# Horner's form with the bare square, and a second m turned out of PSUM, in a matrix square root kernel

## The chip, the cores and the metric

The kernel runs on one core of a Trainium2 chip. The metric is the device time of one execution in microseconds (us), lower is better. Engines are called as in the profile: PE is TensorE (with PEld for its weight loads), DVE is VectorE, ACT is ScalarE, POOL is GpSimd, SP is SyncE, which here only issues DMAs.

## What is computed

The input x has shape (32, 32, 128, 128): 32 images of 32 channels, each channel a 128 x 128 matrix. Layer 0 normalises groups of two channels, and then takes a matrix square root of every channel by five coupled Newton-Schulz steps; layer 1 normalises again and convolves by way of a spectrum. The change is in layer 0:

```python
normA = jnp.sqrt(jnp.sum(A2 * A2, axis=(1, 2)))
Y = A2 / normA[:, None, None]
Z = jnp.broadcast_to(I, A2.shape)
for _ in range(NUM_ITER):
    T = 0.5 * (3.0 * I - jnp.matmul(Z, Y))
    Y = jnp.matmul(Y, T)
    Z = jnp.matmul(T, Z)
sA = Y * jnp.sqrt(normA)[:, None, None]
...
x = x + _L0_conv_ref(_gn(x))
x = x + _L1_conv_ref(_gn(x), L1_conv_weights1, L1_conv_weights2)
```

## The kernel before

**Groups and lanes.** The work of layer 0 is cut into 256 groups of four channels, so a tile of a group is 128 x 512 float32. Each group is one generator, `newton`, which issues some instructions and yields. Up to eight generators (lanes) are under way; the main loop goes round all lanes, one step of each in a round, so that the instructions of eight groups are interleaved on every engine. Every instruction is kept in the order in which the program issues it. A new far group starts every 23/8 = 2.875 rounds (`FAR`). `yield from rest` is two rounds.

**Near and far.** The kernel has no five steps but two quartic polynomials and a final factor. With m the current matrix, a quartic q(m) is evaluated; y = q m; the second m is q y; another quartic of it follows; and then the products of the end. Images 1 to 18 are "far" (144 groups), the others "near" (112 groups, `near_quartic`, which uses PE transposes). Only the far groups are changed.

**The far quartic before.** `far_quartic(m, mb, v, more)` takes m, its transpose mb, and v, a multiple of the identity minus m, which POOL made ahead. TensorE makes the square from mb and m (a product takes its left factor transposed). DVE adds a multiple of the square, from PSUM, to v. The second product needs the transpose of that v as a factor. It is made in two parts: DVE's `transpose` turns every 32 x 32 block (tile `turn`, four buffers in turn), and four DMAs from SP's queue put the blocks of rows into their places in tile `w`. After two rests (four rounds) TensorE multiplies v and w, and DVE adds mb, which POOL has replaced by `eye_q` minus mb, to give q.

**Between the two quartics.** ACT takes y and, two rounds later, the second m out of PSUM (tile `my` holds both side by side). Two rounds later, `transposed(m)` lets TensorE transpose the four matrices of m, ACT copies them into `mb`, and POOL makes v. Two rounds on, the second quartic starts.

**What else runs beside it.** ACT issues the loads of x (`b`, `xt`, and `xs` for the statistics of coming images), SP the stores of the result (`mid`), of spectra (`xs<-spec`) and the `w<-turn` DMAs. DVE also makes the statistics. The later stage of the kernel does the products of layer 1 and the inverse transforms, with the near groups of images 19 to 31 beside them. All instructions pass through one helper, so that the profile gives them all line L89; they are told apart by tiles.

Of the kernel before, what the change touches and what calls it, by code (L numbers as in the profile page):

```python
# [31 lines left out]
ALU = mybir.AluOpType  # L32
# [4 lines left out]
P = 128  # L37
# [11 lines left out]
MS = 1 / QR  # L49
EYE = QD * MS * MS  # L50
QF = EYE / (36 / 16)

SV = MS / 4.5
SQ = MS / 8.625
EYE_V = 3.375 * SV
EYE_Q = 24.609375 * SQ
QS = 16 * SQ
FIRST = GROUPS[0] - 1
MORE = FIRST * 8 + 6
NB = 8  # L60
# [34 lines left out]
def conv_preact_kernel(  # L95
# [19 lines left out]
    nc.vector.tensor_scalar_mul(eye1[:, 0, :], ident, EYE)  # L115
    eye = eye1.to_broadcast([P, 4, P])
    eyes = []
    for n, f in (("v", EYE_V), ("q", EYE_Q)):
        e = const.tile([P, 1, P], F32, name=f"eye_{n}")
        nc.vector.tensor_scalar_mul(e[:, 0, :], ident, f)  # L120
        eyes.append(e.to_broadcast([P, 4, P]))
    eye_v, eye_q = eyes
    avg_mean = const.tile([P, P], F32, name="avg_mean")
    nc.vector.memset(avg_mean, -1.0 / 512)

# [97 lines left out]
    def prep(bs, made):  # L223

        n = len(bs)
        nc_, ng = n * C, n * G
        first_b = bs[0]
        st = small.tile([P, ng, 6], F32, tag="a_st", name=f"a_st{first_b}", bufs=2)
        tiles = []
        parts = [(b, i) for b in bs for i in range(C // 4)]  # L230

        ahead = 3 if first_b else 8

        def load(k):
            b, i = parts[k]
            if first_b or i < 4:
                t = stp.tile([P, 2, 2 * P], F32, tag="xs", name=f"xs{b}_{i}")
            else:
                t = four("turn", True).rearrange("p (j c) x -> p j (c x)", j=2)
            src = xs_in[b, :, 2 * i : 2 * i + 2].rearrange("p g h c -> p g (h c)")  # L240
            kept(nc.scalar.dma_start(out=t, in_=src))
            tiles.append(t)

        for k in range(ahead):
            load(k)
        yield
        for k in range(len(parts)):
            for j in range(2):
                nc.vector.bn_stats(st[:, 2 * k + j, :], tiles[k][:, j, :])
            yield  # L250
            if k + ahead < len(parts):
                load(k + ahead)
        ms = small.tile([P, ng], F32, tag="a_ms", name=f"a_ms{first_b}")
        nm, d = yield from moments(st, ms, "a")
        yield from pause
        pq = bank()[:, 0, 0:nc_]
        nc.tensor.matmul(pq, avg_mean, d.rearrange("p g c -> p (g c)"), start=True, stop=True)
        if not first_b:
            warm(5)

        v = small.tile([P, nc_ + ng], F32, tag="a_v", name=f"a_v{first_b}")
        nc.vector.tensor_scalar_mul(v[:, 0:nc_], pq, -512 / (P * P))
        yield
        vg = small.tile([P, ng], F32, tag="a_vg", name=f"a_vg{first_b}")
        nc.vector.tensor_reduce(
            vg, v[:, 0:nc_].rearrange("p (g c) -> p g c", c=2), AX.X, ALU.add
        )
        nc.vector.tensor_scalar(v[:, nc_:], vg, 0.5, EPS, ALU.mult, ALU.add)
        yield
        s = small.tile([P, nc_ + ng], F32, tag="a_r_s", name=f"a_r_s{first_b}", bufs=2)  # L270
        yield from root(v, nc_ + ng, s)
        iv = small.tile([P, nc_ + ng], F32, tag="a_inv", name=f"a_inv{first_b}")
        nc.vector.reciprocal(iv, s)
        yield

        sc = small.tile([P, nc_], F32, tag="a_sc", name=f"a_sc{first_b}", bufs=2)
        nc.vector.tensor_scalar_mul(sc, iv[:, 0:nc_], MS / P)
        off = small.tile([P, ng, 2], F32, tag="a_off", name=f"a_off{first_b}", bufs=2)
        nc.vector.tensor_tensor(
            off,  # L280
            sc.rearrange("p (g c) -> p g c", c=2),
            nm[:, :, None].to_broadcast([P, ng, 2]),
            ALU.mult,
        )
        off = off.rearrange("p g c -> p (g c)")
        sn = small.tile([P, nc_], F32, tag="a_t_s", name=f"a_t_s{first_b}", bufs=3)
        for k, b in enumerate(bs):
            g, c = slice(k * G, k * G + G), slice(k * C, k * C + C)
            made[b] = (nm[:, g], sc[:, c], off[:, c], sn[:, c])
        yield  # L290
        nn = small.tile([P, ng, 2], F32, tag="a_d", name=f"a_n{first_b}")
        nc.vector.tensor_tensor(
            nn,
            s[:, 0:nc_].rearrange("p (g c) -> p g c", c=2),
            iv[:, nc_:, None].to_broadcast([P, ng, 2]),
            ALU.mult,
        )
        nn = nn.rearrange("p g c -> p (g c)")
        for far in sorted({is_far(b) for b in bs}):
            of = [k for k, b in enumerate(bs) if is_far(b) == far]  # L300
            c = slice(of[0] * C, of[-1] * C + C)
            f = EYE_Q * QS if far else EYE * QF
            nc.vector.tensor_scalar_mul(nn[:, c], nn[:, c], P * (1.5 / f) ** 2)
        yield
        yield from root(nn, nc_, sn)
        yield
# [6 lines left out]
    def four(tag, more):  # L313
        n, m = rooms[tag]
        shape = [P, 4, 2, P] if tag == "my" else [P, 4, P]
        if more:
            turns[tag] += 1
            if turns[tag] % (n + m) >= n:
                return early.tile(shape, F32, tag=tag + "_early", name=tag, bufs=m)
        return sets.tile(shape, F32, tag=tag, name=tag, bufs=n)  # L320
# [15 lines left out]
    def blocks(t):  # L336


        return t.rearrange("p c x -> p (c x)").rearrange("p (a c j) -> p a c j", a=4, c=4)

    def minus(eye, m, t):

        nc.gpsimd.tensor_tensor(t, eye, m, ALU.subtract)
        return t

    def products(lhsT, rhs):
        ps = bank()
        for j in range(4):
            nc.tensor.matmul(ps[:, j, :], lhsT[:, j], rhs[:, j], start=True, stop=True)
        return ps  # L350
# [67 lines left out]
        yield from rest  # L418
        return q

    def far_quartic(m, mb, v, more):

        ps = products(mb, m)
        nc.vector.scalar_tensor_tensor(v, ps, 1 / (4.5 * MS), v, ALU.mult, ALU.add)
        t = four("turn", more)
        nc.vector.transpose(blocks(t), v.rearrange("p c (i b) -> p b c i", b=4))
        w = four("w", more)
        into = w.rearrange("p c x -> p (c x)").rearrange("p (a x) -> p a x", a=4)
        for a in range(4):
            src = t[32 * a : 32 * a + 32].rearrange("p c x -> p (c x)")  # L430
            kept(
                nc.sync.dma_start(
                    out=into[:, a], in_=src.rearrange("p (b x) -> p b x", b=4)
                )
            )
        minus(eye_q, mb, mb)
        yield from rest
        yield from rest
        ps = products(v, blocks(w).rearrange("p a c j -> p c a j"))
        q = plus(ps, SQ / SV**2, mb, "q", more)  # L440
        yield from rest
        return q

# [2 lines left out]
    def newton(g, sn, xt, m, mb, v, far, more):  # L446


        qf, et, eye_t = (QS, EYE_Q, eye_q) if far else (QF, EYE, eye)
        q = yield from far_quartic(m, mb, v, more) if far else near_quartic(m, mb, more)  # L450
        my = four("my", more)
        y = my[:, :, 0, :]
        nc.scalar.mul(y, products(q, m), 1 / (MS * qf))
        yield from rest
        m = my[:, :, 1, :]
        nc.scalar.mul(m, products(q, y), MS / qf)
        yield from rest
        mb = taken(transposed(m), "mb", more)
        if far:
            v = minus(eye_v, m, four("v", more))  # L460
        yield from rest
        q = yield from far_quartic(m, mb, v, more) if far else near_quartic(m, mb, more)
        both = [bank().rearrange("p (j k) x -> p j k x", k=2) for _ in range(2)]
        for j in range(4):
            nc.tensor.matmul(both[j // 2][:, j % 2], q[:, j], my[:, j], start=True, stop=True)
        w, y = four("t", more), four("y4", more)
        for h in range(2):
            nc.scalar.mul(w[:, 2 * h : 2 * h + 2, :], both[h][:, :, 1, :], 1 / (MS * qf))
        for j in range(4):
            c = 4 * g + j  # L470
            nc.scalar.mul(y[:, j, :], both[j // 2][:, j % 2, 0, :], sn[:, c : c + 1])
        yield from rest
        t = plus(products(w, q), -0.5 * et / (1.5 * qf), eye_t, "t", more)
        yield from rest
        nc.vector.tensor_tensor(xt, products(t, y), xt, ALU.add)
        if not todo and lanes.count(None) == LANES - 1:
            warm(2)
        yield
# [707 lines left out]
```

## Time and profile before

| | us |
|---|---|
| median of three runs | 3018.24 (3017.86 to 3018.54) |
| profiled execution, own time | 3016.65 |
| its span | 3014.70 |
| PE busy in 90 to 1554 us (far stage) | 1452.46 of 1464 |
| DVE busy there | 1256.10 |
| POOL busy there | 1056.15 |
| ACT busy there | 884.59 |
| share of the 16 DMA engines there | 0.58 |

The page gives busy time, share of the span and instructions of each engine, then the span in 40 slices, one digit each for tenths of busy time. Groups of instructions are written as output <- inputs, with the shapes, then the count, the busy time and the mean length of one in ns, and behind the second bar the idle time of the engine just before them and what ended it. Waits are written as engine, tile, what was waited for: total us, times, longest. In a timeline each line has a start, a length and what ran; SPq is SP's queue of DMA issues. The stretch view has busy time, with the number of instructions in brackets, for each engine, and then the granted clock, the share of the DMA engines and GB/s.

### The profile page before, as it was taken

To read this page: it belongs to the slowest core of one execution; us is meant where nothing else is said; L and a number is where in the kernel's file an instruction comes from. 1 tells how busy PE (TensorE), PEld (TensorE's weight loads), DVE (VectorE), ACT (ScalarE), POOL (GpSimd) and SP (SyncE) were. 2 spreads that over 40 slices of the span, in tenths; PEclk is the share of its full clock that TensorE was granted. 3 is DMA by queue.
4 is the path that set the end of the run, shared out by engine and by line. 5 is a ranking of instruction groups with operands and counts; after the bars stand their busy time and mean duration, and the time that the engine had idled before them with its cause. 6 is when DMAs were issued, how large, how long until landed. Compare 5 with 4: busy or idle time off the path is not lost.

```text
span 3014.7 us, 73315 instructions
## 1 busy us (share of the span) xinstructions
PE 2897.6 (96%) x27112; PEld 2689.0 (89%) x27112; DVE 2321.8 (77%) x4262; ACT 1652.1 (55%) x4187; POOL 1995.8 (66%) x2308
## 2 busy tenths in 40 slices
PE   7999999999999999999999999999989999999995
PEld 7899999999999999999999889888878899888884
DVE  7778898989888888889876645777886767776564
ACT  4566666566565656566554445455544544665452
POOL 4676777777777767777765434787777763678352
PEclk9999999999999999999999999999999999999997
DMA  5465655556565656565633566777877737676576
GB/s 176 135 176 145 171 163 153 167 152 180 134 192 135 192 131 195 142 183 140 190 102 99 158 209 208 257 247 254 271 235 245 252 121 225 203 242 216 175 230 242
DMA packets 442482, 560.91 MB, mean 186 GB/s; under 512 B 99344, under 2 KB 260112, under 8 KB 442128
## 3 DMA queue, kind: packets, MB, share of 16 engines
q1 hardware_dynamic: 328512, 347.77, 38.7%
q10 hardware_dynamic: 113616, 208.45, 22.2%
q8 instruction: 218, 3.57, 0.5%
q14 instruction: 136, 1.11, 0.1%
HBM read 326.93 MB, written 153.62 MB: 159 GB/s over the span
## 4 chain that ended last, share of the span: by engine, by line
PE 71%; POOL 8%; DVE 7%; DMA 7%; issue 5%; SPq 1%; ACT 1%; ACTq 0%; POOLq 0%; DVEq 0%
PE ps L89 71%; POOL yt L89 3%; POOL r L89 2%; POOL x L89 1%; POOL fold L89 1%; DMA yt<-mid 1%; SPq L89 1%; DVE turn L89 1%; DVE root L89 1%; DMA w<-turn 1%; DMA out<-yt 1%; DVE v L89 1%; DVE yt L89 1%; DVE a_d L89 1%; DMA xs<-in_xs 1%
## 5 line engine op out<-in xcount | busy, mean ns | idle before, releaser
L89 PE MATMUL ps<-my,q 128*128 128x128 f32 (+1 forms) x4096 | 747.0, 330 | 16.6 <-DVE q L89 9.9
L89 PEld LDWEIGHTS ps<-my,q 128*128 128x128 f32 x4096 | 623.0, 192 | 67.7 <-issue 7.4
L89 PE MATMUL ps<-w,v 128*128 128x128 f32 x4096 | 555.4, 279 | 19.6 <-DVE w L89 15.3
L89 ACT ACTIVATE b<-b,a_off,a_sc 128x128 f32<-128x128 f32 x1024 | 469.7, 491 | 166.2 <-issue 57.0
L89 ACT ACTIVATE my<-ps 128x512 f32<-128x512 f32 x512 | 306.2, 599 | 428.3 <-PE ps L89 408.9
L89 POOL TENSOR_TENSOR fold<-xt 128x256 f32<-128x256 f32 x512 | 363.4, 731 | 261.5 <-DVE xt L89 248.9
L89 PEld LDWEIGHTS ps<-w,v 128*128 128x128 f32 x4096 | 502.9, 193 | 32.5 <-DVE w L89 13.9
L89 POOL TENSOR_TENSOR yt<-yt,d 128x512 f32<-128x512 f32 x244 | 306.5, 1279 | 223.2 <-ACT d L89 195.5
L89 ACT ACTIVATE t<-ps 128x256 f32<-128x256 f32 x512 | 192.0, 381 | 311.7 <-PE ps L89 298.4
L89 DVE STREAM_TRANSPOSE turn<-v 128x512 f32<-128x512 f32 x288 | 326.1, 1132 | 9.9
L89 POOL TENSOR_SCALAR x<-xt,a_nm,a_sc 128x128 f32<-128x128 f32 x736 | 321.4, 450 | 15.6 <-DVE a_sc L89 15.4
L89 POOL TENSOR_TENSOR mb<-eye_q,mb 128x512 f32<-128x512 f32 x144 | 184.0, 1278 | 197.8 <-ACT y L89 139.2
L89 ACT ACTIVATE y<-ps,a_t_s 128x128 f32<-128x128 f32 x1024 | 290.4, 374 | 0.0
L89 POOL TENSOR_TENSOR v<-eye_v,x 128x512 f32<-128x512 f32 x144 | 184.0, 1278 | 143.8 <-ACT x L89 136.7
L89 PE MATMUL ps<-q,t 128*128 128x128 f32 x2048 | 273.9, 277 | 4.3 <-ACT t L89 3.7
L89 PE MATMUL ps<-x,b 128*128 128x128 f32 x2048 | 277.7, 279 | 0.0
L89 PE MATMUL ps<-x,q 128*128 128x128 f32 x2048 | 274.7, 277 | 3.0 <-DVE w L89 2.0
L89 DVE SCALAR_TENSOR_TENSOR v<-ps,v 128x512 f32<-128x512 f32 x288 | 195.1, 678 | 104.5 <-PE ps L89 101.8
L89 PE MATMUL ps<-y,t 128*128 128x128 f32 x2048 | 274.5, 277 | 0.1
L89 PE MATMUL ps<-my,mb 128*128 128x128 f32 x2048 | 272.2, 276 | 0.0
L89 PEld LDWEIGHTS ps<-my,mb 128*128 128x128 f32 x2048 | 257.9, 192 | 9.6 <-issue 1.6
L89 PEld LDWEIGHTS ps<-x,q 128*128 128x128 f32 x2048 | 249.4, 192 | 14.1 <-issue 8.4
(131 smaller groups left out, 5074.9 us busy)
## 6 DMA issues: line engine op xcount, KB each, us to landing
w<-turn SPq DMA_DIRECT2D x1152, 64.0 KB
b<-in_x ACTq DMA_DIRECT2D x256, 256.0 KB
xt<-in_xt ACTq DMA_DIRECT2D x256, 256.0 KB
mid<-xt SPq DMA_DIRECT2D x256, 256.0 KB
yt<-mid SPq DMA_DIRECT2D x128, 512.0 KB
xs<-in_xs ACTq DMA_DIRECT2D x252, 256.0 KB
out<-yt SPq DMA_DIRECT2D x115, 512.0 KB
plain<-in_wk SPq DMA_DIRECT2D x34, 512.0 KB
```

The costliest lines, as they stand in the source:

```text
L89: return self.tc.keep_in_program_order(issue(*args, **kw))
```

## The change

The polynomial's constants change. Before, the second factor was a shifted v, so that v itself had to be turned; now it is the bare square, which is turned straight out of PSUM, ahead of the sum into v. So `transpose` reads PSUM instead of SBUF. The second m is no longer transposed by TensorE and copied by ACT: DVE turns it out of PSUM too, after ACT has taken m from the same bank, and four DMAs put it into `mb`, 32 columns of each of the four matrices at a time, where w gets 128 contiguous columns. This starts two rounds earlier than the transposes did. The turned second m is left without ACT's factor, so that the second quartic has its own identity (`eye_p`), factor and scale. The number of rounds of a far group is the same.

```diff
-SV = MS / 4.5
-SQ = MS / 8.625
-EYE_V = 3.375 * SV
-EYE_Q = 24.609375 * SQ
-QS = 16 * SQ
+EYE_V = 3 * MS
+EYE_Q = 36 / 39 * MS
+QS = 16 / 39 * MS
+TURNED = QS / MS
...
-    for n, f in (("v", EYE_V), ("q", EYE_Q)):
+    for n, f in (("v", EYE_V), ("q", EYE_Q), ("p", EYE_Q * TURNED)):
...
-    eye_v, eye_q = eyes
+    eye_v, eye_q, eye_p = eyes
...
-            f = EYE_Q * QS if far else EYE * QF
+            f = EYE_Q * QS * TURNED**2 if far else EYE * QF
...
-    def far_quartic(m, mb, v, more):
+    def across(ps, more, into):
...
-        ps = products(mb, m)
-        nc.vector.scalar_tensor_tensor(v, ps, 1 / (4.5 * MS), v, ALU.mult, ALU.add)
         t = four("turn", more)
-        nc.vector.transpose(blocks(t), v.rearrange("p c (i b) -> p b c i", b=4))
-        w = four("w", more)
-        into = w.rearrange("p c x -> p (c x)").rearrange("p (a x) -> p a x", a=4)
+        nc.vector.transpose(blocks(t), ps.rearrange("p c (i b) -> p b c i", b=4))
         for a in range(4):
             src = t[32 * a : 32 * a + 32].rearrange("p c x -> p (c x)")
             kept(
-                nc.sync.dma_start(
-                    out=into[:, a], in_=src.rearrange("p (b x) -> p b x", b=4)
-                )
-            )
+                nc.sync.dma_start(out=into(a), in_=src.rearrange("p (b x) -> p b x", b=4))
+            )
+
+    def far_quartic(m, mb, v, more, f, eye_q):
+
+        ps = products(mb, m)
+        w = four("w", more)
+        across(ps, more, lambda a: w.rearrange("p c x -> p (c x)")[:, P * a : P * a + P])
+        nc.vector.scalar_tensor_tensor(v, ps, 1 / (9 * MS * f), v, ALU.mult, ALU.add)
         minus(eye_q, mb, mb)
         yield from rest
         yield from rest
         ps = products(v, blocks(w).rearrange("p a c j -> p c a j"))
-        q = plus(ps, SQ / SV**2, mb, "q", more)
+        q = plus(ps, 9 / (39 * MS**2), mb, "q", more)
         yield from rest
         return q
...
-        qf, et, eye_t = (QS, EYE_Q, eye_q) if far else (QF, EYE, eye)
-        q = yield from far_quartic(m, mb, v, more) if far else near_quartic(m, mb, more)
+        qf = QS if far else QF
+        if far:
+            q = yield from far_quartic(m, mb, v, more, 1.0, eye_q)
+        else:
+            q = yield from near_quartic(m, mb, more)
...
-        nc.scalar.mul(m, products(q, y), MS / qf)
-        yield from rest
-        mb = taken(transposed(m), "mb", more)
+        ps = products(q, y)
+        nc.scalar.mul(m, ps, MS / qf)
         if far:
+            mb = four("mb", more)
+            across(ps, more, lambda a: mb[:, :, 32 * a : 32 * a + 32])
+            yield from rest
             v = minus(eye_v, m, four("v", more))
-        yield from rest
-        q = yield from far_quartic(m, mb, v, more) if far else near_quartic(m, mb, more)
+            yield from rest
+            qf, et, eye_t = QS * TURNED, EYE_Q * TURNED, eye_p
+            q = yield from far_quartic(m, mb, v, more, TURNED, eye_p)
+        else:
+            yield from rest
+            mb = taken(transposed(m), "mb", more)
+            yield from rest
+            et, eye_t = EYE, eye
+            q = yield from near_quartic(m, mb, more)
```

## The prediction

> **What bounds the kernel now.** I read the page's sections 1 and 2 first, then busy time by stretch, then groups by form, then SP's waits, all of the stage that the change touches. That stage runs from the first `turn` (89.6 us) to the last (1553.3 us): 144 far groups in 1464 us, and in its even middle part (300 to 1300 us) 100 groups in 1000 us, so 10.0 us a group.
>
> ```profile
> PE 2897.6 (96%) x27112; PEld 2689.0 (89%) x27112; DVE 2321.8 (77%) x4262; ACT 1652.1 (55%) x4187; POOL 1995.8 (66%) x2308
> PE   7999999999999999999999999999989999999995
> ```
> ```profile
> core 0: us, PE busy (x) PEld busy (x) DVE busy (x) ACT busy (x) POOL busy (x), PEclk, DMA share, GB/s
> 700.00:900.00 200.00, 198.82 (x1674) 188.57 (x1673) 174.91 (x318) 120.36 (x308) 145.12 (x160) 1.00 0.59 164
> 1100.00:1300.00 200.00, 199.28 (x1682) 189.08 (x1681) 170.38 (x299) 121.67 (x313) 145.53 (x160) 1.00 0.57 156
> 2000.00:2200.00 200.00, 193.87 (x1747) 175.22 (x1746) 156.16 (x290) 106.55 (x281) 154.66 (x178) 1.00 0.80 263
> ```
>
> A busy PE proves little by itself[...]; but weight loads fill 94% too (189 of 200), the clock is granted in full, and the chain of waits inside 300 to 1300 us is 86.9% "PE ps". So TensorE is the limit of this stage. Second is VectorE: 170 to 175 of 200, or 8.64 us of each 10.0. ScalarE has 6.1, GpSimd 7.3. The third row, of the later stage, shows that a DMA share of 0.80 goes with a PE still 97% busy.
>
> The rows that the change touches (300 to 1300 us, groups by form; then the timeline of the weight loads; then SP's own waits and its issues):
>
> ```profile
> L89 DVE STREAM_TRANSPOSE turn<-v 128x512 f32<-128x512 f32 x200 | 226.5, 1132 | 6.8
> L89 PEld LDWEIGHTS ps<-ident,my 128*128 128x128 f32 x400 | 47.1, 142 | 0.0
> L89 ACT COPY mb<-ps 128x512 f32<-128x512 f32 x100 | 58.5, 585 | 30.5 <-PE ps L89 25.6 <-DVE q L89 2.2 <-DMA w<-turn 1.7
> L89 DVE STREAM_TRANSPOSE u<-ps 128x512 f32<-128x512 f32 x25 | 17.8, 710 | 2.5 <-PE ps L89 2.5
> L89 ACT COPY z<-ps 128x256 f32<-128x256 f32 x26 | 8.4, 375 | 10.4 <-PE ps L89 10.4
> L89 ACT ACTIVATE t<-ps 128x256 f32<-128x256 f32 x198 | 73.5, 379 | 91.2 <-PE ps L89 91.0
> ```
> ```profile
> 802.60 0.47 PEld L89 LDWEIGHTS ps<-ident,my 128*128 128x128 f32 x4
> 803.04 0.97 PEld L89 LDWEIGHTS ps<-w,v 128*128 128x128 f32 x8
> ```
> ```profile
> SPq L89 <- DVE turn L89: 315.5, 93, 7.0
> SPq L89 <- DVE b_v L89: 51.6, 13, 4.7
> SPq L89 <- PE ps L89: 31.4, 98, 0.8
> SPq L89 <- DMA w<-turn: 14.5, 15, 4.9
> ```
> ```profile
> 602.29 2.50 SPq L89 DMA_DIRECT2D w<-turn  x4
> 604.84 0.60 SPq L89 DMA_DIRECT2D mid<-xt  x1
> ```
>
> The reader is to see: the four transposes of a group hold TensorE 0.44 us (802.60 to 803.04); a turn out of SBUF takes 1.13 us, the one block transpose out of PSUM (`u<-ps`) 0.71; SP's waits add up to about 437 us of these 1000 (all rows of that answer), so its issues and the gaps between them take 5.63 us a group: two sets of `w<-turn` at 2.5 us and one `mid<-xt` at 0.54 to 0.60.
>
> [...] The trace speaks against a price there, on ScalarE at least: `z<-ps` reads PSUM in 16-byte steps in 375 ns, the contiguous `t<-ps` of that size takes 379. [...]
>
> **The change part by part**, per far group, against the profiled run (3016.65 us, span 3014.70; the median of the three runs, 3018.24, is 1.6 above it and takes the same difference).
>
> - TensorE loses the 4 transposes of the second m: 0.44 us, times 144 is 63.4 us. They lie on the bound, with nothing beside them; so this is the expected gain. Its bank of PSUM falls away too. Next late is VectorE, then SP.
> - ScalarE loses `mb<-ps`, 0.585 us: 6.1 becomes about 5.5. It has idle time; worth nothing.
> - VectorE has three turns out of PSUM for two out of SBUF. Unknown: the price of a 16-byte step in PSUM. Low end 0.71 (`u<-ps`, contiguous): 8.64 - 2.26 + 2.13 = 8.5 us. High end 1.13, as if the step cost as in SBUF: 9.8. I take 0.71, for the ScalarE row above. At 8.5 of 9.56 us VectorE stays second.
> - The turn now goes ahead of the sum into `v`: w's transfers can start 0.71 us after the product instead of 0.68 + 1.13 = 1.81; `v` is ready 0.71 later, but its product waits for w longer. A gain of slack, not of time. The other constants, the extra eye (one 128x128 multiply at the start) and the norm's factor: nothing.
> - SP gets 4 more issues a group, `mb<-turn`. Their access has one dimension more than w's. Low end 2.5 us a set, as w's. High end: `or<-od` against `ob<-od` (616 and 464 ns medians) puts 150 ns on one more dimension, 3.1 us. SP: 5.63 + 2.5 to 3.1 = 8.1 to 8.7 of 9.56. I take 8.3. Behind a late issue stand the next w set and `mid`.
> - DMA: a row of 32 floats per partition and block, so 128-byte packets, 2048 a group. The store `xs<-spec` has such packets: in the window of 1079.7 to 1081.7 us they were 2070 at 83.6% of 16 engines, 12.9 ns each. 2048 x 12.9 / 16 = 1.65 us a group; the share goes from 0.58 of 10.0 to (5.8 + 1.65) / 9.56 = 0.78, which the later stage bears. [...]
> - Path of the second m: before, PE to ScalarE, transposes two rounds on, ScalarE, product two rounds on. Now it has four rounds (a round is 10.0 / 2.875 = 3.5 us, then 3.3): 13.3 us against 0.6 (ScalarE) + 0.7 (turn) + 2.5 to 3.1 (issues) + 2.2 (landing, the `DMA w<-turn` pieces of the chain last 2.1 to 2.3) = 6 to 7 us, so 6 us for queueing. w has as much.
> - Two added waits. VectorE's turn of m stands behind ScalarE's `my`: queued behind it are turns and sums of other lanes, with 1.0 us of idle time a group to take it. And in the built program each DMA of SP and ScalarE takes one of eight completion semaphores in turn and waits for the DMA eight before it. It was 12 DMAs in 10.0 us, 6.7 us back; it becomes 16 in 9.56, 4.8 us back, with landings of 2.2 us upward. So ScalarE's loads can stand behind SP's sets, and its evacuations behind its loads. The before shows little of it: 14.5 us in 1000 on SP, about 10 on ScalarE. Bounds: nothing, or up to 0.6 us a group, past the gain. I take 0.07 us a group, 10 us: TensorE's idle time in this stage is 11.5 us now (1452.5 busy of 1464), and I let it double.
>
> Sum: -63.4 + 10 = -53; 3018.2 - 53 = 2965 us. Own range 2950 to 2998: from nothing given back with some earlier start, to two thirds of the gain given back.
>
> **The rivals.**
> 1. SP and its ring of eight become the bound (slower). For: SP at 87 to 91% before any wait, three sets per group of which two come close together, TensorE's operands for two of eight products behind it, four `turn` buffers that VectorE must wait for. Against: both paths have 6 us of slack, and the before waited little. Price: 8.7 + 1.6 us of landing waits = 10.3 us a group, +0.3 x 144 = 43: 3061 us. It decides from the point where SP's issues and waits pass 10.0 us a group; between 9.56 and 10.0 it only eats the gain.
> 2. The step in PSUM costs as in SBUF, and VectorE is the bound. [...] Against: `z<-ps`. Price: 9.77 us of work plus 0.4 of waits that stay = 10.2: +25, 3043 us; with no waits left, 2985.
> 3. The gain is eaten by both in part: 9.9 to 10.05 us a group, 3004 to 3025, 3014 in the middle.
> 4. The change doesn't do what it says: excluded for the transposes, which are missing in the changed program's list of TensorE; SP's list has the four new issues a group.
>
> **How the numbers follow.** Forecast 0.58; rival 1 0.22; rival 2 0.12, of which 0.08 slower, 0.02 the same and 0.02 faster; rival 3 0.08, of which 0.03 faster, 0.03 the same, 0.02 slower. About 0.2% (6 us) is what a measurement of this kernel can tell from no change. Faster 0.58 + 0.02 + 0.03 = 0.63, the same 0.05, slower 0.22 + 0.08 + 0.02 = 0.32. The range starts at 2948 (all of the gain, and a little of the startup) and reaches into rivals 1 and 2, to 3060, which leaves out half of rival 1 and the forecast's edges, under 0.2. The forecast's own range stands beside it: 2950 to 2998.
>
> **What would show each step.** Right: the stretches of 200 us hold 20.9 groups instead of 20, PE still at 199; `ps<-ident,my` 448 instead of 1024; `turn<-ps` at 0.71 us; VectorE near 177 of 200; `mb<-turn` issues at 0.60 to 0.75 us and SP's wait for `turn` at a third of before; DMA share 0.75 to 0.8. Wrong: `turn<-ps` over 1 us; SP with hardly a wait for `turn` and long ones for DMAs; ScalarE's `my` or `b` waiting for `mb<-turn`; PE below 195 of 200 with "DMA mb<-turn" or "DVE turn" as releaser. The forecast fails if any of these costs TensorE 0.44 us a group.

## The result, and the profile after

The changed kernel takes 3039.67 us (median of 5 runs, 3030.63 to 3042.62), the one before, on the same chip, 3018.54 (3017.86 to 3020.63). The ratio is 1.0066, with a 95% interval of 1.0049 to 1.0083: slower by 21 us, where 53 us of gain were forecast. The profiled execution took 3030.63 us, 9 under the median, so its trace shows rather too little of the loss; its span is 3028.5.

First the page's sections 1 and 2 of the kernel after, then its busy time by stretch, in the columns that the prediction's fence has.

```profile
PE 2856.4 (94%) x26536; PEld 2636.7 (87%) x26536; DVE 2271.7 (75%) x4407; ACT 1567.5 (52%) x4043; POOL 1995.5 (66%) x2308
PE   7999999999999999999999999999989999999996
```
```profile
700.00:900.00 200.00, 189.43 (x1537) 177.40 (x1536) 161.60 (x329) 105.84 (x285) 141.75 (x156) 0.99 0.75 187
1100.00:1300.00 200.00, 190.90 (x1562) 179.72 (x1561) 162.49 (x314) 108.94 (x290) 143.53 (x158) 1.00 0.74 183
2000.00:2200.00 200.00, 193.96 (x1736) 175.21 (x1735) 156.42 (x292) 107.06 (x280) 156.74 (x177) 0.99 0.78 256
300.00:1300.00 1000.00, 954.87 (x7803) 897.99 (x7803) 814.06 (x1602) 541.54 (x1440) 715.51 (x789) 0.99 0.74 185
```

TensorE has lost its transposes, yet it works less of each stretch: 189 of 200 us, where it was 199. The tenths of section 2 don't show it, as 95% is a 9 too. The last `turn` ends the stage at 1567.3 us, 14 later than before; the later stage (2000 to 2200) is as it was. From one `t` of a group to the next the mean is 10.17 us (10.01 before), with 98.3 groups in 1000 us. So TensorE is busy 954.87 / 98.3 = 9.71 us a group and idle 0.46. Before it was 995.62 / 99.9 = 9.97 and 0.04. Without the 0.44 of the transposes 9.53 should be left: 0.18 us of the loss hide inside "busy", and 0.42 are new idle time.

A part of the 0.18 is the granted clock. From 300 to 1300 us it was 1.00 throughout before. After, it falls to half in four stretches of 3.41 us, and each begins 0.5 to 1.2 us after TensorE has come back from a pause of 2.0 to 3.6 us. The longest such pause and the stretch behind it, in the same columns:

```profile
855.57:859.12 3.55, 0.00 (x1) 0.04 (x1) 3.55 (x9) 0.00 (x0) 1.67 (x3) 1.00 0.93 293
859.98:863.39 3.41, 3.41 (x19) 3.41 (x18) 1.38 (x2) 3.41 (x11) 0.20 (x1) 0.50 0.67 155
```

The other three begin at 518.65, 549.37 and 1006.76 us. TensorE counts as busy in all four, so they hide 6.8 us of work at full clock at most, 0.07 us a group. Two more pauses over 2 us (2.27 and 2.33 us, at 391 and 1165 us) have no such stretch behind them. The other 0.11 us are not explained.

Of the chain of waits inside 300 to 1300 us, 86.9% was "PE ps" before. Now it is 41.6%, and DMAs and SP's issues make up another third (the line's first entries):

```profile
by line: PE ps L88 41.6%; SPq L88 10.6%; DMA w<-turn 8.8%; DMA mb<-turn 8.5%; DMA mid<-xt 4.4%; DVE turn L88 3.1%; issue 2.7%; DVE v L88 2.2%; DMA xs<-in_xs 1.8%; ACT b L88 1.6%; DVE q L88 1.6%; POOL v L88 1.3%; POOL fold L88 1.1%; DVE root
```

No other engine is full: VectorE has 814 of 1000, fewer than before. The groups by form (300 to 1300 us), SP's own waits, and the waits of all engines, in that order:

```profile
L88 DVE STREAM_TRANSPOSE turn<-ps 128x512 f32<-128x512 f32 x295 | 206.9, 706 | 124.4 <-ACT my L88 71.8 <-PE ps L88 44.6 <-DMA w<-turn 6.5
L88 ACT ACTIVATE b<-b,a_off,a_sc 128x128 f32<-128x128 f32 x396 | 191.4, 495 | 202.5 <-DMA b<-in_x 41.4 <-DMA xs<-in_xs 37.9 <-DMA w<-turn 32.6
```
```profile
SPq L88 <- DVE turn L88: 46.3, 47, 3.0
SPq L88 <- DMA w<-turn: 29.1, 38, 2.5
SPq L88 <- DMA mb<-turn: 13.1, 27, 2.5
```
```profile
ACT b L88 <- DMA xs<-in_xs: 37.9, 9, 5.8
ACT b L88 <- DMA w<-turn: 32.6, 18, 4.7
ACT b L88 <- DMA mb<-turn: 20.7, 12, 3.9
PE ps L88 <- ACT my L88: 12.3, 6, 3.3
PE ps L88 <- DMA mb<-turn: 10.4, 8, 3.5
```

A turn out of PSUM is cheap (706 ns, as taken). SP hardly waits for `turn` any more, 46 us for 315, and more for DMAs, 47 us (all rows) for 18. And ScalarE waits for landings that its instruction doesn't need: `b` is computed from `b` and two small tiles of statistics (`a_off`, `a_sc`) and reads neither `w` nor `mb` nor `xs`. In the trace of before "ACT b" waits 8.7 us for `w<-turn` and 4.7 for `xs`. All of ScalarE's idle time that ends with a landing adds up to 163 us in 1000, where it was 27. TensorE's own pauses are 44.5 us in this list: 16.0 end with ScalarE (12.3 of them with `my`), 15.7 with a landing (10.4 with that of `mb`), 10.3 with VectorE. What stands ahead of such a `b` on ScalarE is an issue of a load. The chain of waits after has one such place whole (start in us, length in us, what):

```profile
341.12 5.00 DMA w<-turn
346.12 0.02 issue
346.14 4.00 DMA mid<-xt
350.14 0.02 issue
350.16 0.33 ACTq L88
350.49 0.05 issue
350.54 0.49 ACT b L88
351.03 0.14 ACTq L88
351.17 0.24 ACT x L88
351.42 0.39 ACT b L88
351.80 0.39 ACT x L88
352.19 0.38 ACT b L88
352.57 0.49 ACT my L88
353.06 0.04 issue
353.10 2.94 PE ps L88 x24
```

A store of a result (`mid`) isn't issued until a `w` has landed; a load on ScalarE isn't issued until that store has landed; ScalarE's evacuations stand behind the load, and TensorE behind the evacuation `my`. None of these needs the other's data. The trace's records of DMAs in the program's order (worked out from the issues and the completions) say what joins them: each is the eighth after the other.

```
issue   what           released by            the DMA eight before   landed
346.14  SP  mid<-xt    w<-turn (346.12)       w<-turn                346.12
350.16  ACT xs<-in_xs  mid<-xt (350.14)       mid<-xt                350.14
351.03  SP  w<-turn    w<-turn (351.02)       w<-turn                351.02
398.44  ACT xt<-in_xt  w<-turn (398.37)       w<-turn                398.37
```

The place shown isn't the only one. In each of the six waits of TensorE for `my` (12.3 us in all), worked out from the trace in the same way, a load `xs` ahead of that evacuation stands eight places behind a store `mid` and is issued 0.02 us after that has landed.

ScalarE itself stands still in such a wait: it sits idle for 4.26 us ahead of the `b` at 350.54, until a load `xs` that was held by the store `mid` has been issued (0.33 us, at 350.16).

### The profile page after: what moved, and what is told of

The parts are those of the page before. It is cut to its first block, busy times and chain, and to the rows that moved or that the text cites. A ratio compares the mean times of both kernels' runs of the same rounds, so it can differ in the third digit from the quotient of the medians.

```text
span 3028.5 us, 73234 instructions
## 1 busy us (share of the span) xinstructions
PE 2856.4 (94%) x26536; PEld 2636.7 (87%) x26536; DVE 2271.7 (75%) x4407; ACT 1567.5 (52%) x4043; POOL 1995.5 (66%) x2308
## 4 chain that ended last, share of the span: by engine, by line
PE 51%; DMA 17%; DVE 10%; POOL 9%; issue 5%; SPq 5%; ACT 2%; ACTq 1%; DVEq 0%; POOLq 0%
PE ps L88 51%; SPq L88 5%; DMA w<-turn 4%; DMA mb<-turn 3%; POOL yt L88 3%; DMA yt<-mid 2%; DMA mid<-xt 2%; POOL r L88 2%; POOL fold L88 2%; DVE turn L88 2%; POOL x L88 2%; DMA xs<-in_xs 1%; DVE v L88 1%; DVE yt L88 1%; DVE q L88 1%
## 5 line engine op out<-in xcount | busy, mean ns | idle before, releaser
L88 DVE STREAM_TRANSPOSE turn<-ps 128x512 f32<-128x512 f32 x432 | 302.8, 705 | 178.4 <-ACT my L88 102.1
L88 POOL TENSOR_TENSOR mb<-eye_p,mb 128x512 f32<-128x512 f32 x144 | 184.0, 1278 | 133.1 <-PE ps L88 130.9
L88 PEld LDWEIGHTS ps<-q,t 128*128 128x128 f32 x2048 | 251.1, 193 | 9.2 <-ACT t L88 7.3
```

Source lines behind the costliest of these rows:

```text
L88: return self.tc.keep_in_program_order(issue(*args, **kw))
```

## The experiments

All times are medians, with the ratio to the kernel before, run beside it on the same chip, and its 95% interval. The kernel before has 3016 to 3020 us in these series, so that a few us between two experiments mean nothing. Each expectation names its theories in its own words; in most, theory 1 is that the number of DMAs on the rotation of eight semaphores is what costs. A statistic that is used below was worked out in the same way for each trace, from 300 to 1300 us; the last column is the sum of ScalarE's waits that end with a landing. Each row is one execution; that of the 512-byte packets took 3020.32 us, 12 above its median, that of the half-turned kernel 3011.01, 13 above.

```
                         period  DMAs    mean in  mean     ScalarE's issues held    ScalarE idle until
                         us      /group  flight   landing  by the DMA eight before  a landing, us
before                   10.01   12.1    3.7      3.07     21%                       27
after                    10.17   16.1    5.2      3.31     60%                      163
Horner alone              9.95   12.1    3.8      3.14     15%                       27
half turned               9.90   14.1    4.8      3.39     26%                       44
mb in 512-byte packets    9.98   16.1    5.2      3.19     59%                      118
four unread, 2 KB        10.15   16.2    4.7      2.94     38%                       77
four unread, 64 KB       10.18   16.2    5.0      3.17     46%                       88
four unread, plain       10.29   16.1    5.3      3.41     53%                      113
one unread, 256 KB       10.01   13.1    4.3      3.26     30%                       50
way through memory       11.09   10.1    4.0      4.39     14%                       34
```

**The two halves of the change apart.** The first keeps the bare square out of PSUM, and has the second m transposed by TensorE as before:

```diff
-            mb = four("mb", more)
-            across(ps, more, lambda a: mb[:, :, 32 * a : 32 * a + 32])
+            mb = taken(transposed(m), "mb", more)
```

> Only the first half of the change: the bare square is turned out of PSUM in both quartics; the second m goes through TensorE's transposes and ScalarE's copy as before (12 DMAs a group, TensorE at 10.0 us a group). All theories: TensorE stays the bound, 3010 to 3020 us. Over 3025 us would say that the new order in the quartic costs something by itself.

Measured: 2998.45 us, 0.9943 (0.9926 to 0.9961). The line of its stretches and the shares of its chain, for 300 to 1300 us:

```profile
300.00:1300.00 1000.00, 999.73 (x8386) 949.99 (x8386) 763.94 (x1533) 613.23 (x1572) 733.19 (x807) 1.00 0.57 162
```
```profile
by line: PE ps L88 98.1%; DMA w<-turn 0.9%; ACT b L88 0.3%; DMA b<-in_x 0.2%; ACT x L88 0.1%; DVE v L88 0.1%; ACT my L88 0.1%; issue 0.1%; ACTq L88 0.1%; DVE turn L88 0.0%; DVEq L88 0.0%
```

TensorE is never idle here. The half that the prediction called slack alone gains 18 us (with VectorE at 764 instead of 864), more than any theory expected; the half that takes 63 us of work off TensorE costs about 40 us on top of it (3040 - 2998 = 41 by the medians, 37 by the ratios).

**Only every second far group turned**, the others transposed by TensorE:

```diff
-        if far:
+        if far and g % 2:
...
+        elif far:
+            yield from rest
+            mb = taken(transposed(m), "mb", more)
```

> The bare square in all far groups, but only every second group has its second m turned by VectorE and DMAs; the others keep TensorE's transposes. 14 DMAs a group instead of 16, TensorE's work 9.75 us a group, SP's 7.1. Theory 1 (SP and the ring of eight, full at 16): most of half the gain of 63 us comes on top of the Horner half's 2998 us: 2965 to 2985 us. If every turned group costs more than it saves by its own path (latency of the second m), it lies between 2998 and the changed kernel: 3005 to 3025 us.

Measured: 2997.68 us, 0.9935 (0.9914 to 0.9956). With 14 DMAs a group the work of half the transposes, 32 us, is saved and given back: against Horner alone, 1 to 2 us are no difference. The time lies between the two ranges that were expected and decides for neither.

**VectorE behind ScalarE.** The turn of the second m is placed ahead of ScalarE's evacuation from the same bank:

```diff
+        if far:
+            mb = four("mb", more)
+            across(ps, more, lambda a: mb[:, :, 32 * a : 32 * a + 32])
         nc.scalar.mul(m, ps, MS / qf)
```

> The changed kernel, with VectorE's turn of the second m ahead of ScalarE's reading of the same bank, so that VectorE waits for TensorE alone and ScalarE waits for VectorE. Theory 3: VectorE's wait for my (72 us in 1000) goes, time 2975 to 3015. Theories 1 and 2: within 10 us of the changed kernel.

Measured: 3046.43 us, 1.009 (1.0065 to 1.0116). With the wait that the prediction named first gone, ScalarE's `my` waits 174 us in 1000 for VectorE's `turn`, and the time is no better. One wait is put in another's place here, so this doesn't show that the first cost nothing; it shows that taking it away alone doesn't help.

**DMAs without the change.** The kernel before gets four more DMAs a group from SP, of the second m into a tile that nobody reads: 64 KB each, 512 bytes a packet, over 128 partitions.

```diff
+            for a in range(4):
+                kept(nc.sync.dma_start(out=junk[:, a], in_=m[32 * a : 32 * a + 32]))
```

> The kernel before, with four more DMAs per far group, out of the second m into tiles that nobody reads, in 512-byte packets. Theory 1 (16 instead of 12 DMAs a group go through SP's queue and the ring of eight completion semaphores): TensorE's work is still 10.0 us a group, so the time rises by a large part of what the change lost, to 3035 to 3080 us, and ScalarE's and SP's waits for DMAs rise as in the changed kernel. Theory 2 (the 128-byte packets of mb) and theory 3 (VectorE queues behind ScalarE's second m): within 5 us of before.

Measured: 3040.74 us, 1.0082 (1.0067 to 1.0097). TensorE's work, VectorE's and ScalarE's are those of before, and 25 us are lost. Then the same bytes from 32 partitions to the same 32 (`out=junk[rows], in_=m[rows]`), and the whole tile in one DMA (`out=junk, in_=m`):

> The kernel before with four more unread DMAs of 64 KB a far group, as in the earlier run with four unread DMAs, but from 32 partitions to the same 32 partitions, which SP issues in about 0.32 us instead of 0.6. Ring of eight alone (16 DMAs a group): as much slower as that run, +15 to +30 us against before. SP's issue time: about half, +5 to +15 us. Bytes alone: +25 us, as the bytes are the same.

> The kernel before with one more unread DMA of 256 KB a far group: the bytes and packets of four, but one place in the ring and one issue of 0.32 us. Ring or SP's issue time: within 8 us of before. Bytes and the load of the DMA engines: +20 us or more.

Measured: 3059.13 us, 1.0133 (1.0108 to 1.0158), and 3017.47 us, 0.9998 (0.9984 to 1.0012). The same 256 KB a group cost nothing as one DMA and 25 to 41 us as four. So it isn't the bytes. The plain ones land in 3.79 us, the four of the run before in 3.35. Their issue on SP took 0.62 us, not the 0.32 that was expected, so that a shorter issue was not tried. Last, four of one row, 2 KB each (`rows = slice(32 * a, 32 * a + 1)`):

> The kernel before, with four unread DMAs a group from the second m as in the run with 64 KB each, but of one row of 2 KB each, so that 16 DMAs a group stand on the rotation of eight semaphores and next to nothing is moved. Theory 1 (the number of DMAs on the rotation, or SP's issue of them, is what costs, whatever they carry): 3035 to 3060 us, as the 64 KB ones gave. Theory 2 (what costs is the time that the DMAs take, each short one beside the others' data, so number times landing time): within 10 us of before, 3008 to 3028 us, because a 2 KB DMA lands sooner and gives its semaphore back sooner.

Measured: 3027.51 us, 1.0041 (1.0027 to 1.0054). They land in 2.45 us and cost 11 us, against 25 and 41. SP issues one in 610 ns (median), and in 602 and 625 in the other two: with SP's issue time the same, the loss goes with the time in flight, as theory 2 has it. What the number costs by itself, SP's 2.4 us of issues a group included, is 11 us at most.

**The packets of mb.** In the changed kernel, `mb` gets 128 contiguous columns, as `w` does. This makes the second quartic's transposed factor another matrix, so that the second half of the square root isn't computed; the instructions are the same.

```diff
-            across(ps, more, lambda a: mb[:, :, 32 * a : 32 * a + 32])
+            across(ps, more, lambda a: mb.rearrange("p c x -> p (c x)")[:, P * a : P * a + P])
```

> The changed kernel, with each block written as 128 contiguous columns of mb instead of 32 columns of each of four matrices, so 512-byte packets as for w. The blocks go to wrong matrices, so the transposed factor of the second quartic is another; all instructions stay. Theory 2: landing falls from 3.7 to about 2.7 us, DMA share from 0.75 to about 0.68, time to 2975 to 3010. Theories 1 and 3: within 10 us of the changed kernel (3030 to 3043).

Measured: 3008.43 us, 0.9981 (0.9969 to 0.9992). `mb` lands in 3.23 us instead of 3.67, and 31 us (26 by the ratios) of the 40 that the second half costs are back, with 16 DMAs a group still. The time lies in theory 2's range and outside that of theory 1, which counts DMAs alone. So sooner landing alone, at the same count, is worth most of that cost; but the 63 us of the transposes don't come through here either.

**Which place in the queues?** First, ScalarE's loads are held back until just ahead of SP's next set; then until just after it; the first of these also for the half-turned kernel and for the one with four unread DMAs of 64 KB.

```diff
-            fetch(*fetches.pop(0))
+            later.append((fetch, fetches.pop(0)))
...
+        flush()
```

> The changed kernel; ScalarE's loads of x are held back in the program until just before the next set of four turn DMAs, so that the DMA eight places before them is older when ScalarE comes to them. Nothing else moves, and the loads run groups ahead. Theory 1a (ScalarE stands behind SP's sets in the ring of eight, and with it the second m, the turn and TensorE): ScalarE's waits for DMAs fall, time 2970 to 3020 us. If the number of DMAs hurts in another way (landing[...]): within 8 us of the changed kernel.

> As the run with the loads before the sets, but they are issued right behind a set of four turn DMAs, so that the DMA eight places before them is that of the set before. Theory 1a: slower than the run with the loads before the sets by 20 us or more. Otherwise the two are alike within 8 us.

> Every second far group turned, and the loads held back until before the sets. Theory 1a: 2965 to 2988 us, the fastest so far. Otherwise 2995 to 3005.

> The kernel before with four unread DMAs a far group, and the loads held back until before the sets of w. Theory 1a: at least half of the 25 us that the four unread DMAs cost is gone, 3018 to 3030 us. Otherwise 3036 to 3045.

Measured: 3056.38 us, 1.0125 (1.0107 to 1.0143); 3058.18, 1.0126 (1.0106 to 1.0145); 3016.25, 0.9995 (0.9985 to 1.0005); 3052.61, 1.0114 (1.0087 to 1.0142). In the changed kernel both places are worse, and equally so, and in the other two kernels nothing is gained; theory 1a misses all four times. But the edit didn't do what it was for: ScalarE's waits for landings, 163 us in 1000 in the changed kernel, are 181 and 144 in the first two, and VectorE waits 55 and 48 us for `xs`, 18 in the changed kernel, so loads held back come late on either side of a set. That the loads' place against SP's sets is what matters has found no support; what a ScalarE that isn't held would give was not seen here.

**Loads from SP** in the half-turned kernel (`nc.sync` for `nc.scalar` at `b`, `xt` and `xs`), so that ScalarE never holds an evacuation behind an issue:

> As the run with half of the groups turned, with the loads of x on SP's queue instead of ScalarE's. SP has 7.1 + 1.05 us of issues a group. If the loss comes from ScalarE standing behind DMAs of SP in the ring, this is faster than the run with half the groups turned, by 5 to 20 us; if SP's own queue is the limit, slower by as much.

Measured: 3028.81 us, 1.0034 (1.0023 to 1.0045). ScalarE no longer waits for any landing (44 us in 1000 in the half-turned kernel), and yet the time is 31 us longer, where 5 to 20 us of gain were expected if that wait were the loss. The wait moves, from ScalarE to VectorE's statistics:

```profile
DVE a_st L88 <- DMA xs<-in_xs: 94.1, 36, 5.6
```

**Fewer DMAs by pairs**: the changed kernel's statistics loads in 512 KB instead of 256, 15.6 DMAs a group.

> The changed kernel with the loads for the statistics (xs) in pairs of 512 KB, so that they take 0.5 instead of 1 place a group in the ring: 15.5 DMAs, the bytes as before, one of them ScalarE's. Theory 1: 5 to 20 us faster than the changed kernel. Bytes or path: within 5 us.

Measured: 3045.75 us, 1.0089 (1.0071 to 1.0107). Half a DMA less a group gains nothing, where theory 1 expected 5 to 20 us; the loads of twice the size land in 4.37 us, those of before in 3.79, and as many are in flight (5.1).

**The stores from GpSimd**, which is off the rotation: of the changed kernel, of the half-turned one, of Horner alone.

```diff
-        kept(nc.sync.dma_start(out=mid[b][:, 4 * g : 4 * g + 4, :], in_=xt))
+        kept((nc.gpsimd if is_far(b) else nc.sync).dma_start(out=mid[b][:, 4 * g : 4 * g + 4, :], in_=xt))
```

> The changed kernel, with the far groups' stores of the result (mid) issued by GpSimd, whose DMAs have no place in the ring of eight: 15 DMAs a group in it instead of 16, and SP has 0.6 us a group less to issue. Theory 1 (the ring's count): 10 to 30 us faster than the changed kernel, 3010 to 3030 us. If the loss is in the path of the second m alone: within 8 us of it. If GpSimd becomes the bound (7.3 us[...]): slower.

> Every second far group turned, with the stores on GpSimd: 13 DMAs a group in the ring, TensorE's work 9.75 us a group. Theory 1: 2970 to 2988 us, faster than half turned alone (2998) and than the Horner half alone (2998). Path of the second m alone: 2990 to 3000.

> The Horner half alone with the stores on GpSimd: 11 DMAs a group in the ring. TensorE is busy all the time there, so the ring has nothing to give: 2990 to 3000 us under theory 1. Slower than 3003 us would say that DMAs on GpSimd cost something by themselves, to be taken off the other two runs.

Measured: 3111.15 us, 1.0294 (1.027 to 1.0318); 3062.91, 1.0149 (1.0124 to 1.0175); 3005.57, 0.9956 (0.9941 to 0.9971). These don't decide: another effect came with them. The groups by form, of the first of these kernels and then of the changed one:

```profile
L88 DVE TENSOR_SCALAR a_t_s<-root 128x64 f32<-128x64 f32 x6 | 18.7, 3124 | 0.2
L88 DVE TENSOR_TENSOR b_inv<-b_r 128x1 f32<-128x1 f32 x12 | 21.8, 1816 | 0.4
```
```profile
L88 DVE TENSOR_SCALAR a_t_s<-root 128x64 f32<-128x64 f32 x6 | 3.7, 618 | 0.2
L88 DVE TENSOR_TENSOR b_inv<-b_r 128x1 f32<-128x1 f32 x12 | 2.9, 244 | 0.4
```

Small VectorE instructions take 2.5 us and 1.6 us longer (every one of these `a_t_s` starts while GpSimd is issuing a store), and the sums of other lanes are queued behind them: TensorE waits 43.1 us for VectorE's `q` there, 7.7 in the changed kernel.

**Ten DMAs a group.** The whole change, but each set of four goes by a scratch tile in device memory: one plain DMA out, and two rounds later one DMA back in the turned order.

```diff
-        for a in range(4):
-            src = t[32 * a : 32 * a + 32].rearrange("p c x -> p (c x)")
-            kept(
-                nc.sync.dma_start(out=into(a), in_=src.rearrange("p (b x) -> p b x", b=4))
-            )
+        hop = hops.tile([P, 4 * P], F32, name="hop", tag="hop")
+        kept(nc.sync.dma_start(out=hop, in_=t.rearrange("p c x -> p (c x)")))
+        return hop
...
         yield from rest
+        src = hop.rearrange("(a r) (b x) -> (r b) a x", a=4, b=4)
+        kept(nc.sync.dma_start(out=w, in_=src))
         yield from rest
```

> Each set of four DMAs is replaced by two: SP writes the whole tile turn to a scratch tile in device memory in one plain DMA, and two rounds later one DMA reads it back into w or mb in the turned order (512-byte runs for w, 128-byte runs for mb). A far group so has 10 DMAs on the rotation of eight semaphores in place of 16 (12 before), and TensorE has its 63 us less. But 768 KB more are moved a group, and SP's second DMA waits for the first one's landing, two rounds (about 6.6 us) later. Theory 1 (the number of DMAs in flight together is what the change pays for): the far period falls from 10.17 to below 9.9 us and the time to 2950 to 2990 us, ScalarE's issues held by the DMA eight before fall from 60% to under 25%. Theory 2 (the 128-byte packets and the sets' landing as such, or VectorE's and ScalarE's order of work, are what it pays for, whatever the number of DMAs): 3030 us or more, a period of 10.1 or more with PE waiting for DMA w<-hop or mb<-hop.

Measured: 3178.9 us, 1.054 (1.0515 to 1.0565), a period of 11.09 us. Its stretch, two rows of its waits, and one of SP's own:

```profile
300.00:1300.00 1000.00, 888.93 (x7127) 836.49 (x7128) 733.43 (x1452) 503.83 (x1316) 657.15 (x722) 0.98 0.85 240
```
```profile
PE ps L88 <- DMA mb<-hop: 53.3, 22, 3.8
PE ps L88 <- DMA w<-hop: 50.2, 31, 4.5
```
```profile
SPq L88 <- DVE turn L88: 445.4, 231, 6.7
```

ScalarE's issues are held as seldom as expected (14%), but TensorE now waits for the operands themselves. Two landings (3.7, then 4.6 to 5.3 us) stand in one path, and SP, which waits in order for each `turn` of the lanes (445 us), issues the second DMA late. The share of the DMA engines is 0.85 and the granted clock 0.98. A miss of theory 1's expectation: the lower count didn't help here, where the transfers got slower and the path longer.

**What the runs show together.** Shown are three things. The chain shows the link, in each of the six places where TensorE waits for `my` (one DMA held by the landing of the DMA eight before, an evacuation behind it, TensorE behind that). The unread DMAs show that more of them cost time with no work changed, and more where they land later (11 us at a landing of 2.45 us, 25 at 3.35, 41 at 3.79). The 512-byte packets show that landing sooner, in 3.23 us for 3.67, brings most of the second half's cost back (26 to 31 of 40 us). How often ScalarE's issues are held doesn't order the kernels: that of the 512-byte packets is held as often as the changed one (59% and 60%) and loses less. How long ScalarE is idle until a landing fits better, with 118 us in 1000 there and 163 in the changed kernel, 77, 88 and 113 with the unread fours; but the way through memory, with 34, loses most, by its own path.

Not shown is how much of the loss this rotation of eight makes. The edits that were to relieve it (half turned, loads in other places, loads on SP, loads in pairs, stores from GpSimd, the way through memory) all missed what was expected of it, and most brought another wait or a longer path. TensorE's pauses that end with a landing itself (15.7 us in 1000) are as large as those that end with ScalarE (16.0). A kernel with more semaphores in the rotation wasn't tried. No kernel here beat both Horner alone and the half-turned one, which stand level at 2998 us, 0.6% under the kernel before.

## Why the prediction was wrong

- **The step that failed** is the term of the two added waits: "I take 0.07 us a group, 10 us". By the periods, what came on top of TensorE's remaining work was 10.17 - 9.56 = 0.61 us, 88 us over 144 groups, which is the prediction's own upper bound ("up to 0.6 us a group, past the gain"). How much of it the two waits make stays open: TensorE's pauses behind ScalarE are 0.16 us a group, those that end with a landing itself 0.16, those behind VectorE 0.10, the halved clock takes up to 0.07, and 0.11 are not explained. The mechanism was named, "ScalarE's loads can stand behind SP's sets, and its evacuations behind its loads", and the chain shows it in those words. Its size was taken from TensorE's idle time before, 11.5 us, doubled, and "about 10 on ScalarE" counts the waits for `w` alone: with those for `mid`, `xs` and the rest they were 27 us in 1000. And the rotation was read with the shortest landing, 2.2 us, against 4.8 us back; the mean of all DMAs was 3.07 us already, and those in the piece of the chain shown above took 4 and 5. With 3.3 us, 16 DMAs in 10.17 us are 16.1 x 3.31 / 10.17 = 5.2 in flight of eight on average, with sets issued in bunches of four and eight. At that average 60% of ScalarE's issues were held by the DMA eight before, where it was 21% at 3.7. Two of the prediction's signs of being wrong came up: `b` waits for `mb<-turn` (20.7 us), and PE is below 195 of 200 with "DMA mb<-turn" among its releasers.
- Of the two waits, VectorE's behind ScalarE is real (71.8 us), but taking it away, with the reverse wait in its place, gave 3046. It isn't shown to have cost anything.
- **TensorE's transposes**: gone, and the 0.44 us with them, as forecast; they were on the bound then and not after.
- **The turn out of PSUM**: 0.71 us taken, 706 ns measured. The rival of the dear step in PSUM is out. That the step is what made the turn out of SBUF last 1132 ns was the author's estimate; no run here shows it.
- **The turn ahead of the sum**, priced as "A gain of slack, not of time": wrong the other way. Horner alone gained 18 us and brought TensorE from 995.6 to 999.7 us of 1000. Between the two traces, 19.4 us apart, 5.0 are won by the 30th group, 7.5 from there to the 120th, 2.6 up to the last, and the rest behind the far stage; why, outside the even part, wasn't taken apart.
- **SP**: an issue of `mb<-turn` has a median of 632 ns, 2.5 us a set, the low end, and SP's issues with their gaps take 8.5 us a group for the 8.3 taken. SP isn't full (about 160 of 1000 us are waits; the 437 before are 439 when added up, which changes nothing) and didn't become the bound by its work, as rival 1 had it; the ring in rival 1's name did damage, and the period, 10.17 us, came near the 10.3 of that rival. That is luck in part: the price has 1.6 us of landing waits on SP, of which there are 0.48 us a group.
- **DMA**: a share of 0.78 forecast, 0.74 to 0.75 measured; that is 7.5 us of each group in both, with 251,333 packets under 512 bytes in 1000 us for 43,899 before, so the price of the 128-byte packets was right. But "which the later stage bears" drew a wrong comfort from it. The share says how busy the engines are; what counted, by the run with 512-byte packets, was how long each transfer kept its place (3.67 us for `mb`, 3.23 there). The 128-byte packets, worth 26 to 31 us, had been priced as share alone.
- **Paths of w and mb**, 6 us of slack each: TensorE waits 10.4 us for `mb` in 1000, so the slack was used up at times, by issues that came late and landings of up to 5 us.

## What to carry to other kernels

Before moving work from a full engine to DMAs, multiply their number in a period by their mean landing time (all DMAs, not the quickest) and compare that with how many may be in flight; at 3.7 of eight this kernel hardly waited, at 5.2 it lost more than the 63 us it had saved. No threshold was measured, and the way through memory, with 4.0 in flight, shows that a low figure isn't enough. In these traces an issue that waited in ScalarE's queue held the compute instructions behind it (4.26 us ahead of one `b`), so look in the waits for an instruction that waits for a DMA whose tile it doesn't read. And try the halves of a change apart: here the one to which the sum gave no gain made all of it.

## What was not expected of the hardware

- 256 KB a group more cost nothing as one DMA (0.9998) and 0.8 to 1.3% as four of 64 KB; four of 2 KB cost 0.4%.
- After a pause of TensorE of 2.0 to 3.6 us, the granted clock was half for 3.41 us, from 0.5 to 1.2 us after its return, in four of six cases after the change; with the plain unread DMAs, two pauses of 2.1 and 2.5 us had no such stretch (clock 1.00 from 300 to 1300 us).
- In the changed kernel with its stores issued by GpSimd, VectorE's `a_t_s` (128x64) took 3124 ns instead of 618, and a 128x1 instruction 1816 instead of 244.
- A DMA's issue on SP cost the same 0.60 to 0.63 us for 2, 64 and 256 KB of these copies (medians 610, 602 and 625, and 628 ns).
- VectorE's turn of blocks that reads PSUM in 16-byte steps (`turn<-ps`) takes 706 ns, as a contiguous one (`u<-ps`) does (708), where the same from SBUF (`turn<-v`, before) took 1132.
